# A vision block chain with a selective scan: the last stage of each image moves, through DRAM, into the scan of the next image

## The chip, the core and the metric

The kernel runs on one core of a Trainium2 chip. The time is device microseconds from start to end of one launch, the median of several runs. Five engines work side by side, each through its own instructions in order: PE (matrix multiply; PEld is its weight load), DVE (vector engine), ACT (scalar engine), POOL (GpSimd) and SP, which here only issues DMAs. They wait for one another by semaphores.

## The reference

Eight images of 56 x 56 positions (L = 3136 tokens) with 192 channels go through four blocks, each added to its input. All is float32.

1. A gated unit: group norm, then three projections to 576 channels; two Toeplitz products along the image's rows and columns; the gate; a projection back.
2. Window attention: 7 x 7 windows, shifted by 3, six heads, with a bias table.
3. A 3 x 3 convolution per channel.
4. A two-dimensional selective scan. A projection makes 2 x 384 channels, x and z; x goes through a 3 x 3 convolution and a Silu. The tokens are then scanned in four orders (rows and columns, forwards and backwards), each with 16 states a channel:

```
h[t] = exp(delta[t] * A) * h[t-1] + delta[t] * x[t] * B[t]
y[t] = sum over the 16 states of C[t] * h[t]
```

The four y and D * x are summed. The **last stage** takes this sum: layer norm over the 384 channels, times Silu(z), a projection to 192 channels, and the block's input is added. That is the output.

## The kernel before, in words

A first part (the Toeplitz products, and the first blocks of image 0) takes 3091 us. The rest, 18,104 us, is a single program over the scans of all eight images; all other work is laid between the scan's instructions.

**The scan.** An image has four scan orders, called slots, in the order 2, 3, 0, 1; a slot has seven chunks of 448 tokens (`CH`), a chunk three groups of 128 channels (`d`), a group eight steps `k` of two states each. One step is a *pair*: there are 672 pairs an image and 5,376 in all. The loop over `pairs` writes each one's instructions:

- POOL multiplies du by B into a ring buffer (`inject`, L1124), two pairs ahead;
- ACT makes the decays exp(delta * A) into PSUM (`decay`, L1141, two activations), sets the start values (L1131) and keeps the last states (L1163);
- DVE scans (L1150);
- the result times C (`times_c`, L1156) goes to POOL for even k and to DVE for odd k;
- PE adds the states up with an identity matrix (`add_up`, L1171);
- once per group, DVE adds y into `ysum`, a tile with all tokens of the image (`sums`, L1181 and L1183). It stands at k = 4 of the group after.

SP loads B and C (`load_bc`, L1092), x (`load_xc`, L1097) and delta (`load_delta`) ahead of use.

**The front.** Everything up to the inputs of the scan is the generator `front(b)`: `gate` (block 1), `attention`, `conv2`, `inner` (first projection, convolution and Silu of block 4, in three groups) and `steps` (delta, B and C, in 14 portions of two orders and seven chunks, with a Softplus at L1000). The front of image b + 1 runs while image b is scanned; the next starts as soon as one is through. `gate`, `inner` and `steps` use Silu or Softplus, which need another function table on ACT: a table load stands before and after.

**The finish.** The last stage is the generator `finish(b, j)`, one for each chunk j. It takes `y` straight from `ysum`, makes the mean on PE (L1024), subtracts it on DVE into `yc` in the tile `slab_f` (L1031), and then, for each half of the chunk: the square on ACT (L1036), its mean on PE (L1024), Ln and Exp on ACT (L1041, L1042), a multiply on POOL (L1046), scale and bias on ACT (L1049), a multiply by z on POOL (L1053), the projection on PE (L1058), the sum on DVE (L1066) and the store. SP loads z and the block's input (L1043, L1044) and stores the output (L1067).

**The planner.** `Parts` lays both generators between the pairs. Each yields where it may be put off, with the PSUM banks that it holds and needs (two are free for this) and a time until its load is there. The planner keeps a clock for POOL, ACT, DVE and PE from fixed costs and a list of costs for each kind of client (`"front"`, `"finish"`). After each pair, `step` resumes a client as long as its next piece fits into room that the scan leaves on ACT, PE and DVE (`fits`); a finish is asked before the front. All of this happens when the program is built; the order of each engine is then fixed. Where a piece must be out by some point, the loop calls `parts.step(anything, ...)`, which sets no limits.

**Where the finish stands.** Chunk j of slot 1 is the last part of `ysum` to be complete. Five steps into the chunk after it, the loop forces out what remains of the finish before and adds `finish(pb, pj)`:

```
if i and pslot == 1 and (d, k) == (0, 5):
    while ending in parts.clients:
        parts.step(anything, ending)
    ending = parts.add(finish(pb, pj), "finish")
```

Slot 1 runs backwards, so j goes from 6 to 0, one finish every 24 pairs, from pair 534 of an image to pair 5 of the next. Slot 2 of the next image writes columns across all of `ysum`; at pair 12 the loop therefore forces the last finish on until it has read `ysum` (`while ending.at < 3`).

Of the kernel before, what the change touches and what calls it, by code (L numbers as in the profile page):

```python
# [15 lines left out]
F32 = mybir.dt.float32  # L16
# [7 lines left out]
L = H * W  # L24
# [3 lines left out]
CH = 448  # L28
NCH = L // CH
# [4 lines left out]
ND = DI // 128  # L34
# [5 lines left out]
WP = W + 2  # L40
RUN = 8 * WP
SLOT = NG * (CH + 1) + HALF


class Meter:
# [43 lines left out]
def model(ctx: ExitStack, tc: tile.TileContext, a: dict, out: bass.AP):  # L89
    nc = tc.nc  # L90
    B = out.shape[0]
    const = ctx.enter_context(tc.tile_pool(name="const", bufs=1))
    dram = ctx.enter_context(tc.tile_pool(name="dram", bufs=1, space=DRAM))
# [23 lines left out]
        for n, shape in (("xc", [128, ND, L]), ("bc", [64, L]))  # L117
    )
    dl_d = [[dram.tile([128, ND, L], F32, name=f"dl{s}_{b}") for b in range(B)] for s in range(4)]
    bmask_d = dram.tile([PT_, 4, 6, PT_], F32, name="bmask_d")  # L120
    dg2_d = dram.tile([CP, C // 32, 3, 32], F32, name="dg2_d")
    dg3_d = dram.tile([CP, DI // 32, 3, 32], F32, name="dg3_d")
# [274 lines left out]
    with (  # L397
# [618 lines left out]
        def finish(b, j):  # L1016

            yc, _, sq, rs, x3 = carve(slab_f, 128, (ND, CH), (HALF,), (ND, CH // 2), (CH // 2,), (2, CH // 2))
            x3 = x3[:CP]
            n = CH // 2  # L1020

            def mean(p, src, n):
                for d in range(ND):
                    nc.tensor.matmul(p[:, :n], ones, src[:, d, :], start=d == 0, stop=d == ND - 1)  # L1024

            y = ysum[:, :, j * CH : (j + 1) * CH]
            yield 0, 1
            p = bank()
            mean(p, y, CH)
            yield 1, 0  # L1030
            nc.vector.tensor_sub(yc, y, p[:, :CH].unsqueeze(1).to_broadcast([128, ND, CH]))  # L1031
            for u in range(2):
                yield 0, 0
                tok = slice(j * CH + u * n, j * CH + (u + 1) * n)
                yu = yc[:, :, u * n : (u + 1) * n]
                nc.scalar.activation(sq, yu, AF.Square)  # L1036
                yield 0, 1
                p = bank()
                mean(p, sq, n)
                yield 1, 0  # L1040
                nc.scalar.activation(rs, p[:, :n], AF.Ln, bias=eps5)  # L1041
                nc.scalar.activation(rs, rs, AF.Exp, scale=-0.5)  # L1042
                nc.sync.dma_start(out=sq, in_=z_d[b][:, :, tok])  # L1043
                nc.sync.dma_start(out=x3, in_=blocks(x3_d[b])[:, :, tok])  # L1044
                yield 0, 0
                nc.gpsimd.tensor_mul(yu, yu, rs.unsqueeze(1).to_broadcast([128, ND, n]))  # L1046
                yield 0, 0
                for d in range(ND):
                    nc.scalar.activation(  # L1049
                        yu[:, d, :], yu[:, d, :], AF.Identity, scale=ln_g[:, d : d + 1], bias=ln_b[:, d : d + 1]  # L1050
                    )
                yield 0, 0
                nc.gpsimd.tensor_mul(yu, yu, sq)  # L1053
                yield 0, 1
                p = bank()
                for m in range(2):
                    for d in range(ND):
                        nc.tensor.matmul(  # L1058
                            p[:CP, m * n : (m + 1) * n],
                            w_out[:, d, m * CP : (m + 1) * CP],  # L1060
                            yu[:, d, :],
                            start=d == 0,
                            stop=d == ND - 1,
                        )
                    yield 1, 0
                nc.vector.tensor_add(x3, x3, p[:CP, :CH].rearrange("p (m n) -> p m n", m=2))  # L1066
                nc.sync.dma_start(out=blocks(out[b])[:, :, tok], in_=x3)  # L1067
            yield 0, 0
# [237 lines left out]
        with tc.manual_schedule():  # L1306
            for k in range(NP):
                load_bc(0, k)
            load_delta(0)
            for d in range(ND):  # L1310
                xcs[0, d] = load_xc(0, d)
                times_x(0, d)
            ahead, last = 2, len(pairs) - 1
            parts = Parts()
            run = parts.run

            fed, set_, scanned, taken, summed = ([0.0] * (len(pairs) + ahead + 8) for _ in range(5))

            def feed(g):
                inject(g)  # L1320
                fed[g] = run("P", 1.78, taken[g - 6] if g > 5 else 0.0)

            def take(g):
                times_c(g)
                after = scanned[g], summed[g - 4] if g > 3 else 0.0
                taken[g] = run("P", 1.78, *after) if on_pool(*pairs[g][1:]) else run("D", 1.09, *after)

            def prepare(g):
                decay(g)
                set_[g] = run("A", 1.3, taken[g - 2] if not on_pool(*pairs[g - 2][1:]) else scanned[g - 2])  # L1330

            for g in range(ahead + 2):
                initial(g)
            for g in range(ahead):
                feed(g)
            prepare(0)
            ahead_of, b_next = parts.add(first, "front"), 1
            ahead_of.at, ahead_of.needs = so_far, 1
            ending, anything = None, dict.fromkeys("ADE", 1e9)
            for g, (i, d, k) in enumerate(pairs):  # L1340
                b, slot, j = chunks[i]
                if ahead_of not in parts.clients and b_next < B:
                    ahead_of = parts.add(front(b_next), "front")
                    b_next += 1
                more = i + 1 < len(chunks)
                if more and d == 1 and k == 0:
                    b1, slot1, j1 = chunks[i + 1]
                    while (b1, slot1 // 2, j1) not in made:
                        parts.step(anything, ahead_of)
                    load_delta(i + 1)  # L1350
                    for e in range(2):
                        xcs[i + 1, e] = load_xc(i + 1, e)
                if more and (d, k) == (2, 0):
                    xcs[i + 1, 2] = load_xc(i + 1, 2)
                if more and (d, k) in ((1, 6), (1, 7), (2, 6)):
                    times_x(i + 1, k - 6 if d == 1 else 2)
                    run("P", 0.93)
                pi, pd, pk = pairs[g - 1]
                if g + ahead <= last:
                    feed(g + ahead)  # L1360
                if g and on_pool(pd, pk):
                    take(g - 1)
                if g:
                    keep_state(g - 1)
                    run("A", 0.15, scanned[g - 1])
                if g < last:
                    prepare(g + 1)
                if g + ahead + 2 <= last:
                    initial(g + ahead + 2)
                    run("A", 0.19, taken[g - 2] if g > 1 else 0.0)  # L1370
                scan(g)
                scanned[g] = run("D", 2.02, set_[g], fed[g])
                if not on_pool(d, k):
                    take(g)
                if g and pd == ND - 1 and pi + 1 < len(chunks):
                    load_bc(pi + 1, pk)
                done = (i, d - 1) if d else (i - 1, ND - 1)
                if k == 2 and g > NP and chunks[done[0]][1] == 2:
                    xds[done] = load_xc(*done)
                if i % (4 * NCH) == 0 and b > 0 and (d, k) == (1, 4):  # L1380
                    while ending.at < 3:
                        parts.step(anything, ending)
                if k == 4 and g > NP:
                    sums(*done)
                pb, pslot, pj = chunks[i - 1]
                if i and pslot == 1 and (d, k) == (0, 5):
                    while ending in parts.clients:
                        parts.step(anything, ending)
                    ending = parts.add(finish(pb, pj), "finish")

                n1 = max(parts.t["D"], fed[g + 1], set_[g + 1])
                n2 = n1 + (2.02 if on_pool(*pairs[min(g + 1, last)][1:]) else 3.11)
                parts.step({"A": max(n2, fed[g + 2]) - 0.7, "E": n1 + 5.0, "D": 0.2})
                if g >= 2:
                    add_up(g - 2)
                    summed[g - 2] = run("E", 1.1, taken[g - 2])
            if on_pool(d, k):
                times_c(last)
            for g in (last - 1, last):
                add_up(g)  # L1400
            while parts.clients:
                parts.step(anything)
            sums(i, d)
            drain(finish(b, j))


# [102 lines left out]
```

## Time and profile before

| | |
|---|---|
| median of 3 runs | 21210.55 us (21205.3 to 21239.73) |
| profiled execution, its own time | 21232.23 us |
| its span, first to last instruction | 21230.4 us |
| mean granted PE clock | 0.887 |
| PE busy | 17275.3 us (81%) |
| DVE busy | 15946.5 us (75%) |
| POOL busy | 15628.1 us (74%) |
| ACT busy | 12357.9 us (58%) |
| DMA | 3470.49 MB, mean 163 GB/s |
| scan of images 0 to 6 | 3090.9 to 19334.3 us |
| scan of image 7 | 19334.3 to 21194.7 us |

A line of the profile's groups names the line of the kernel, the engine, the operation, the tile written and those read, the shapes, the number of instructions, their busy time and mean duration, and the idle time of the engine ahead of them with what ended it. A line of the waits says which instruction waited for which, for how long in all, how often, and how long at most. A line of the timeline has start, duration, and in brackets the idle time before. A line for a stretch ends with the granted PE clock, the share of time that the DMA engines were busy, and the rate in GB/s.

### The profile page before, as it was taken

What the parts mean: (1) busy time and instruction counts of PE and PEld (TensorE: products, weight loads), DVE (VectorE), ACT (ScalarE), POOL (GpSimd) and SP (SyncE); (2) the same over time, 40 slices, a digit from 0 to 9 for tenths busy, and PEclk for the clock granted to TensorE, in tenths of its full rate; (3) what the DMA queues carried; (4) which work ended last, traced back from release to release, by engine and by line L of the source; (5) the groups of instructions that cost most, each with busy time, mean ns of one, the idle gap of its engine ahead of it and who ended that gap; (6) DMA issues with size and microseconds to landing.
All of it is one profiled execution on the core that took longest, in us unless ns stands there. A gap on an engine that the chain in (4) does not pass through costs nothing. (4 is left out here: it accounts for less than half of the span.)

```text
span 21230.4 us, 204042 instructions
## 1 busy us (share of the span) xinstructions
PE 17275.3 (81%) x59420; PEld 8921.0 (42%) x59420; DVE 15946.5 (75%) x12633; ACT 12357.9 (58%) x31640; POOL 15628.1 (74%) x9378
## 2 busy tenths in 40 slices
PE   8879669877888788878987898778877898787777
PEld 4667534433443344433543344334433444333333
DVE  2333218986799679977898789867996789779998
ACT  3112236756666566757675667666665767575555
POOL 1222218977788778967897788877886789779999
PEclk9989779988998899988998899988988899888889
DMA  4776665456544655376546654565447554664443
GB/s 99 183 171 159 156 201 164 132 169 187 179 140 139 212 182 150 120 209 194 154 134 183 197 173 130 162 200 171 145 129 218 175 153 129 192 200 147 137 134 128
DMA packets 2562885, 3470.49 MB, mean 163 GB/s; under 512 B 932462, under 2 KB 2514896, under 8 KB 2530930
## 3 DMA queue, kind: packets, MB, share of 16 engines
q1 hardware_dynamic: 2542788, 3340.61, 53.4%
q0 software_dynamic: 18976, 116.82, 1.6%
q8 instruction: 473, 7.75, 0.2%
q14 instruction: 648, 5.31, 0.1%
HBM read 2822.68 MB, written 634.11 MB: 163 GB/s over the span
## 5 line engine op out<-in xcount | busy, mean ns | idle before, releaser
L1171 PE MATMUL ps_y<-hc,ident_sb 128*128 128x448 f32 x21504 | 9973.0, 601 | 772.7 <-POOL hc L1156 694.9
L1124 POOL TENSOR_TENSOR ring<-du,bm 128x896 f32<-128x896 f32 x5376 | 9462.5, 1778 | 677.6 <-ACT ring L1131 381.9
L1141 ACT ACTIVATE ps_a<-delta,A_logs_sb 128x449 f32<-128x449 f32 x10752 | 6860.1, 638 | 378.2 <-DVE ring L1150 122.3
L1171 PEld LDWEIGHTS ps_y<-hc,ident_sb 128*128 128x128 f32 x21504 | 4301.0, 210 | 5071.2 <-issue 3630.9
L1156 POOL TENSOR_TENSOR hc<-ring,cm 128x896 f32<-128x896 f32 x2688 | 4776.2, 1777 | 1946.8 <-DVE ring L1150 914.9
L1150 DVE TENSOR_TENSOR_SCAN ring<-ps_a,ring 128x898 f32<-128x898 f32 x2688 | 5423.9, 2018 | 792.8 <-ACT ps_a L1141 690.0
L1150 DVE TENSOR_TENSOR_SCAN ps_a<-ps_a,ring 128x898 f32<-128x898 f32 x2688 | 5427.6, 2019 | 679.8 <-ACT ps_a L1141 622.8
L1156 DVE TENSOR_TENSOR hc<-ps_a,cm 128x896 f32<-128x896 f32 x2688 | 2934.9, 1092 | 1028.3 <-PE ps_y L1171 798.0
L1163 ACT COPY state<-ps_a 128x2 f32<-128x2 f32 x2687 | 426.8, 159 | 2782.1 <-DVE hc L1156 2773.9
L282 POOL COPY tm<-tr 112x2688 f32<-112x2688 f32 x85 | 406.9, 4791 | 1055.0 <-PE ps_tz L319 507.9
L1131 ACT COPY ring<-state 128x2 f32<-128x2 f32 x4608 | 822.4, 178 | 506.1 <-POOL hc L1156 505.2
L1107 POOL TENSOR_TENSOR du<-delta,xcd 128x448 f32<-128x448 f32 x672 | 661.4, 984 | 360.2 <-DMA xcd<-xc 360.2
L319 PE MATMUL ps_tz<-tzx,tm 112*112 112x112 f32 x4008 | 804.9, 370 | 143.6 <-DMA tzx<-qv 84.2
L319 PEld LDWEIGHTS ps_tz<-tzx,tm 112*112 112x112 f32 x4008 | 760.2, 203 | 174.7 <-issue 107.3
L722 PE MATMUL ps_f<-ident_sb,slab 98*98 98x98 f32 x1344 | 341.3, 327 | 602.5 <-ACT slab L715 602.5
L1163 ACT COPY state<-ring 128x2 f32<-128x2 f32 x2688 | 504.6, 188 | 508.8 <-DVE ring L1150 496.6
L323 DVE COPY tzx<-ps_tz 112x448 f32<-112x448 f32 x501 | 311.5, 623 | 593.9 <-PE ps_tz L319 542.0
L241 ACT ACTIVATE sl<-ps_qv 128x384 f32<-128x384 f32 x600 | 293.3, 491 | 779.5 <-PE ps_qv L240 590.1
L1058 PE MATMUL ps_f<-slab_f,w_out_sb 128*96 128x224 f32 x1320 | 348.7, 408 | 368.9 <-POOL slab_f L1053 366.3
L722 PEld LDWEIGHTS ps_f<-ident_sb,slab 98*98 98x98 f32 x1344 | 203.4, 157 | 1021.2 <-ACT slab L715 802.8
L991 PE MATMUL ps_f<-slab,w_dt_sb 12*128 12x448 f32 x1260 | 441.7, 712 | 219.6 <-ACT slab L983 157.4
L553 PE MATMUL ps_f<-ident_sb,slab 112*96 112x112 f32 x4704 | 529.0, 267 | 110.8 <-DVE slab L561 69.1
(259 smaller groups left out, 17370.3 us busy)
## 6 DMA issues: line engine op xcount, KB each, us to landing
bm<-bc SPq DMA_DIRECT2D x1792, 448.0 KB
cm<-bc SPq DMA_DIRECT2D x1792, 448.0 KB
xcd<-xc SPq DMA_DIRECT2D x840, 224.0 KB
dl<-slab SPq DMA_DIRECT2D x224, 672.0 KB
delta<-dl SPq DMA_DIRECT2D x224, 672.0 KB
tzx<-qv SPq DMA_DIRECT2D x192, 588.0 KB
o<-tzx POOLq DMA_DIRECT2D x192, 588.0 KB, 11.9
slab<-pad SPq DMA_DIRECT2D x483, 232.0 KB
```

The costliest lines, as they stand in the source:

```text
L319: nc.tensor.matmul(po[:, c, :], t[:, c2 + c, :], x[:, :, c1 + c2 + c], start=True, stop=True)
L553: nc.tensor.matmul(p[:CP, t * TT : (t + 1) * TT], ot[:, n % 2, i, t, c % 2 * CP : c % 2 * CP + CP], ident[:TT, :TT], start=i == 0, stop=i ...
L722: nc.tensor.transpose(p[:PT_, e * PT_ : (e + 1) * PT_], S[:, 3 * g + e, :], ident[:PT_, :PT_])
L991: nc.tensor.matmul(held[s][:, :CH], w_dt[row, o, d * 128 : (d + 1) * 128], rc[row, n % 2, :], start=True, stop=True)
L1107: nc.gpsimd.tensor_mul(du[:, 0, :], deltas[i][:, d, 1 : CH + 1], xcs.pop((i, d)))
L1124: nc.gpsimd.tensor_mul(hs[:, :, tokens(i)[0]], dus[i, d].to_broadcast([128, NG, CH]), bms[i, k])
L1131: nc.scalar.copy(in_ring(g)[:, :, tokens(i)[1]], src)
L1141: nc.scalar.activation(dA[:, n, :], deltas[i][:, d, at : at + CH + 1], AF.Exp, scale=negA[:, slot, d, c : c + 1])
L1150: nc.vector.tensor_tensor_scan(h, dA, hs, 0.0, ALU.mult, ALU.add)
L1156: (nc.gpsimd if on_pool(d, k) else nc.vector).tensor_mul(hc, h[:, :, tokens(i)[0]], cms[i, k])
L1163: nc.scalar.copy(states[i][:, d, NG * k : NG * k + NG], h[:, :, tokens(i)[2]])
L1171: nc.tensor.matmul(yps[i, d][:, :CH], ident, hcs[g][:, n, :], start=k + n == 0, stop=k + n == NP + NG - 2)
```

## The change

The finishes of images 0 to 6 no longer stand in the image's own last slot. When a chunk of slot 1 is complete, its part of `ysum` is stored to a DRAM buffer (two buffers, by turns). In the next image, at its pairs 84, 120, 156, 192, 228, 264 and 300, one `finish` of the image before is added, chunks 0 to 6; what remains of the one before is forced out first. Such a finish first loads its chunk from DRAM into `yc` and allows 8.0 us for it; the rest of it is as it was. The wait at pair 12 is gone. Image 7 has no next image: its finishes stay where they were and read `ysum`; they have their own cost list, `"last"`.

```diff
+FINISH, FINISH_EVERY = 84, 36
...
+    y_d = [dram.tile([128, ND, L], F32, name=f"y{q}") for q in range(2)]
...
             y = ysum[:, :, j * CH : (j + 1) * CH]
+            if b < B - 1:
+                y = yc
+                nc.sync.dma_start(out=y, in_=y_d[b % 2][:, :, j * CH : (j + 1) * CH])
+                yield 0, 0, 8.0
             yield 0, 1
             p = bank()
             mean(p, y, CH)
...
-                if i % (4 * NCH) == 0 and b > 0 and (d, k) == (1, 4):
-                    while ending.at < 3:
+                n = g - b * len(pairs) // B - FINISH
+                if b > 0 and n >= 0 and n % FINISH_EVERY == 0 and n // FINISH_EVERY < NCH:
+                    while ending in parts.clients:
                         parts.step(anything, ending)
+                    ending = parts.add(finish(b - 1, n // FINISH_EVERY), "finish")
                 if k == 4 and g > NP:
                     sums(*done)
                 pb, pslot, pj = chunks[i - 1]
                 if i and pslot == 1 and (d, k) == (0, 5):
-                    while ending in parts.clients:
-                        parts.step(anything, ending)
-                    ending = parts.add(finish(pb, pj), "finish")
+                    if pb < B - 1:
+                        tok = slice(pj * CH, (pj + 1) * CH)
+                        nc.sync.dma_start(out=y_d[pb % 2][:, :, tok], in_=ysum[:, :, tok])
+                    else:
+                        while ending in parts.clients:
+                            parts.step(anything, ending)
+                        ending = parts.add(finish(pb, pj), "last")
```

The added lines move the kernel's line numbers: after the change those of the finish from L1031 on, and of the scan, are six higher (the scan is L1156, L1046 is L1052), and the means at L1024 are L1026. The new load is L1031.

## The prediction

> **What bounds the kernel now.** I read the page first (no engine above 81%, and a chain of waits too scattered to name a bound), then how long stretches of the scan take, then who waits inside them. A row of the next view is a stretch: start and end, length, busy time of the scans in it and their number, which is the number of pairs.
>
> ```profile
> 3255.90:19334.20 16078.30, 9345.72 (x4658) 0.90 0.55 167
> 19741.00:20767.10 1026.10, 756.44 (x380) 0.87 0.41 132
> 20773.10:21194.60 421.50, 287.61 (x144) 0.91 0.41 132
> 5565.30:5990.80 425.50, 263.37 (x131) 0.97 0.60 168
> 16859.50:17356.70 497.20, 279.43 (x139) 0.96 0.57 161
> 10523.50:11288.60 765.10, 506.73 (x253) 0.92 0.41 129
> 11288.80:11464.50 175.70, 85.92 (x43) 0.86 0.64 180
> 16038.60:16458.80 420.20, 228.96 (x114) 0.86 0.73 226
> 4629.90:5108.80 478.90, 239.54 (x120) 0.85 0.68 207
> 3096.00:3230.70 134.70, 81.43 (x41) 0.87 0.52 182
> 3230.90:3255.70 24.80, 5.99 (x4) 0.62 1.01 262
> 11898.70:12322.00 423.30, 222.35 (x111) 0.87 0.59 192
> ```
>
> Row 2 is image 7 with neither front nor finish: 1026.1 / 380 = 2.70 us a pair. I call that the floor and count all else as time above it. Row 1, from the first gate to the end of image 6, has 16078 - 4658 x 2.70 = 3502 us above it: seven fronts and 49 finishes. Row 3 holds six finishes alone: 421.5 - 144 x 2.70 = 33 us, 5.5 each.
>
> The other rows show a front's phases, bounded by where their instructions stand among the scalar engine's decays. Gate without a finish (row 4): 425.5 - 131 x 2.70 = 72; with 3.5 of them (row 5): 122, so 14 a finish. Attention (row 6): 82, no finish ever beside it. Conv2 (row 7): 60. Inner without (row 8): 112; with 2.8 (row 9): 155, so 15 each. Steps: half of them without a finish (row 10) 24, the join of three pairs to the next phase (row 11) 17, so 65 in all; with 4.4 (row 12): 124, so 13 each. A straight line through all seven cycles gives gate 75 + 12.6 a finish, inner 119 + 14.1, steps 65 + 14.5; the means of attention and conv2 are 84 and 66. A front alone is then 409 us above the floor, seven are 2863, and 3502 - 2863 = 639 us are the 49 finishes: four stand behind the last front (22 us), the other 45 cost 13.7 each.
>
> Why a finish costs 5.5 alone and 13.7 beside steps: the scalar engine and GpSimd in steps.
>
> ```profile
> 12151.74 0.39 ACT L1042 ACTIVATE slab_f<-slab_f 128x224 f32<-128x224 f32 x1
> 12152.15 1.28 ACT L1000 ACT_TABLE_LOAD   x1
> 12153.44 2.44 ACT L1000 ACTIVATE slab<-slab 128x2688 f32<-128x2688 f32 x1
> 12155.90 1.28 ACT L435 ACT_TABLE_LOAD   x1
> ...
> 12158.58 1.50 ACT L1049 ACTIVATE slab_f<-slab_f,ln_b_sb,ln_g_sb 128x224 f32<-128x224 f32 x3
> ```
>
> ```profile
> 12152.20 1.39 POOL L1046 TENSOR_TENSOR slab_f<-slab_f 128x672 f32<-128x672 f32 x1 [4.76 <-ACT slab_f L1042]
> ...
> 12160.21 1.37 POOL L1053 TENSOR_TENSOR slab_f<-slab_f 128x672 f32<-128x672 f32 x1 [4.89 <-ACT slab_f L1049]
> ```
>
> A Softplus between two table loads (5.0 us) stands in the middle of the finish's chain. GpSimd waits 4.8 and then 4.9 us for the scalar engine, with the scan's own multiplies behind it. The waits of GpSimd in row 12 (four finishes), and in row 3 (six), say the same:
>
> ```profile
> POOL slab_f L1046 <- ACT slab_f L1042: 25.6, 8, 4.8
> POOL slab_f L1053 <- ACT slab_f L1049: 19.9, 4, 5.2
> ```
>
> ```profile
> POOL slab_f L1046 <- ACT slab_f L1042: 0.5, 2, 0.2
> ```
>
> Gate and inner have such blocks too (Silu: 2.45 and 2.82 us between loads of 1.28). Attention has none: its longest scalar instruction, decays aside, is 0.58 us. Busy times there (row 6; PE, PEld, DVE, ACT, POOL):
>
> ```profile
> 10523.50:11288.60 765.10, 633.27 (x2287) 312.91 (x2286) 722.03 (x600) 562.57 (x1779) 691.95 (x413) 0.92 0.41 129
> ```
>
> A pair of 3.02 us has DVE busy 2.85, POOL 2.74, PE 2.50, ACT 2.22: the vector engine is nearly the bound, the others have room.
>
> **The change part by part.**
>
> *Finishes move.* By the changed order of instructions, the seven finishes of images 0 to 5 now stand at pairs 84 to about 330 of the next image, nearly all beside its attention, which stretches from 253 pairs to 273-283. Steps shrink from about 107 pairs to 83, a whole cycle stays near 654, and the last front ends at pair 4591 instead of 4618; with a front's cost counted above the floor, these pairs need no term. Each finish issues what it did: POOL 2 x (1.381 + 1.375) = 5.5 us, ACT 2 x (0.761 + 0.446 + 0.391 + 3 x 0.563) = 6.6, DVE 1.55 + 2 x 0.61 = 2.8, PE 11.8, and six DMAs. Of the 42, two fall into gate (12.6 each = 25); the seven of image 6 go into image 7 at 5.5 = 38. The price of the other 40 is the unknown. Low end 1.5: attention's room over 36 pairs (POOL 10 us, DVE 6) swallows the finish, and only the 28 added pairs run at attention's 0.32 above the floor (9 us over six). High end 14.5, as in steps. I take 6.5: the free 5.5, as there are no long scalar blocks, plus 1 because attention's own reduction waits on the scalar engine that now has 6.6 us more. So 40 x 6.5 + 25 + 38 = 323 against 639: **-316 us**. Ends: 40 x 1.5 gives -516, 40 x 14.5 gives +4.
>
> *A store and a load through DRAM.* 49 of each, 672 KB, 67 MB beside 3470 (1.9%). In the DMA records the equal loads delta<-dl land 6.3 us after issue (middle 80%: 4.7 to 8.8), the equal stores dl<-slab after 5.5, at most 8.8. The planner gives y 8.0 us before its first matmul, so I take 0; if each were 2.9 late (the longest load, 10.9) and PE stood, 142. The store waits on SP for an add issued one pair earlier; behind it on SP stand the front's transfers, later delta and bm. SP waits 6.4 us a time for the softplus output already (677 us in 105), so I take 0, at most one pair each, 132. The first sum of the next image overwrites ysum and must wait for the last store, seven pairs (19 us) behind its issue: 10 to spare; 0, and if SP comes 18 late as it does at its worst, 8 x 7 = 56.
>
> *Planner waits removed* (a finish forced out before the next; the first three parts forced at pair 12): the second half was out 11 to 21 pairs after the first, within the 24, so 0. They order instructions only.
>
> *Two rules of the Trainium skill* stand against parts of this and the sum does not use them. TensorE: Matmul & The Clock Gate (Architectural detail) says that ScalarE, VectorE and GpSimdE are strict FIFO, so a finish's hops between engines would hold what is behind them wherever it stands: 40 x 13.7 + 63 = 611, a gain of only 28. Against it row 3 shows the same hops at 5.5. ScalarE: Activation LUTs (What ACT_TABLE_LOAD costs) puts a switch at 2.66 us with a drain; the Softplus block would be 2 x 2.66 + 2.44 = 7.8 us, and escaping it worth 2.7 us more a finish, some 120 in all. The trace shows 5.0 and no drain, so I leave that out.
>
> **Sum.** The profiled execution took 21232.2 us (span 21230.4): 21232 - 316 = 20916. The median of the runs is 22 below it: **20895**, 1.5% faster. About 0.2%, 42 us, can be told from no change.
>
> **The rivals.**
> 1. *Forecast*, 0.52: 20895.
> 2. *The finish stalls itself*, 0.14: 13.7 each in attention too, 28 gained, 21183. For: PE waits at L1058 for POOL in row 3 as well (37.2 us in six finishes). Against: DVE waited 13 us for PE in all six.
> 3. *Slower: the vector engine becomes the bound in attention*, 0.08. Its reductions hang on scalar and PE, and PE can stand at L1058 up to 7.7 us twice a finish. If both stand on the path: 5.5 + 15.4 = 20.9 each, 40 x 20.9 + 63 = 899, 21471. It decides from (639 - 63) / 40 = 14.4 on. For: DVE 94% busy. Against: room on PE.
> 4. *Steps get no cheaper*, 0.14: they move data at a DMA share near 0.6 and now run in 83 pairs. If their base is 90 (what the last cycle shows with 2.5 finishes, these free), seven times 25 comes back: 21070.
> 5. *Attention swallows it*, 0.12: 1.5 each, 20695.
>
> **How the numbers follow.** Cases 1, 4, 5 and half of 2 are faster by over 0.2%: 0.85; the rest of 2 and of the DMA prices is the same, 0.06; 0.09 slower. The range, 20720 to 21180, leaves out most of 5 and 3 and ends at 2; the forecast's own is 20800 to 21000.
>
> **What would show it.** Right: steps near 83 pairs in 290 us, the waits of L1046 and L1053 on ACT mostly gone, attention with finishes at 3.0 to 3.25 us a pair (at 6.5 each: 280 pairs in about 880), image 7 near 1900 instead of 1860. Wrong: attention above 3.4 a pair, which eats the gain; new waits of DVE for y's store, or of PE for its load; steps still above 3.6 a pair.

## The result, and the profile after

The changed kernel takes 21321.69 us (median of 4 runs, 21316.9 to 21351.62), the kernel before 21214.93 us beside it. The ratio is 1.0051, with a 95% interval of 1.0034 to 1.0069: **slower by half a per cent, some 107 us**, where 1.5% faster was forecast. The profiled execution took 21316.9 us (before: 21232.2).

The first view answers the table of stretches in the prediction: start and end, length, busy time of the scans and their number, which is the number of pairs or one more (a scan that begins just at the edge is counted). It is the changed kernel's.

```profile
3247.97:19017.98 15770.01, 9117.59 (x4545) 0.89 0.56 171
20297.09:20848.81 551.72, 406.14 (x205) 0.85 0.41 134
8073.58:9064.65 991.07, 603.15 (x301) 0.90 0.45 136
14891.41:15911.14 1019.73, 607.09 (x303) 0.89 0.43 131
9605.21:9917.87 312.66, 172.19 (x86) 0.83 0.65 216
19556.15:20221.86 665.71, 429.45 (x216) 0.85 0.44 141
```

Row 1 is all seven fronts: 15770 - 4545 x 2.70 = 3498 us above the floor. Before it was 3474, and 3502 with the four finishes behind the last front. The floor has not moved either (row 2: 551.72 over 204 pairs is 2.70). So seven fronts with 42 finishes beside them cost 24 us more than seven fronts with 45. Rows 3 and 4 are two attentions with their finishes: 3.29 and 3.37 us a pair, where 3.0 to 3.25 was forecast. Row 5 is steps with no finish beside it, 3.64 a pair. Row 6 is image 7 from its pair 84 to 300, with six moved finishes and no front: 665.71 - 216 x 2.70 = 82 us, 13.7 each, where such finishes had cost 5.5.

The waits of the changed kernel (total us, times, longest; three engines and SP's queue) say what is new in the finish:

```profile
POOL slab_f L1052 <- ACT slab_f L1048: 102.7, 49, 11.8
POOL slab_f L1059 <- DMA slab_f<-z: 79.0, 21, 6.9
POOL slab_f L1059 <- ACT slab_f L1055: 50.2, 36, 4.2
...
PE ps_f L1026 <- DMA slab_f<-y: 171.6, 25, 12.4
...
DVE slab_f L1037 <- PE ps_f L1026: 189.9, 32, 13.6
...
SPq L1049 <- PE ps_f L1026: 1370.7, 83, 47.6
```

The same waits in the kernel before:

```profile
POOL slab_f L1046 <- ACT slab_f L1042: 292.1, 80, 10.4
POOL slab_f L1053 <- ACT slab_f L1049: 158.1, 47, 5.2
POOL slab_f L1053 <- DMA slab_f<-z: 31.1, 19, 3.6
...
DVE slab_f L1031 <- PE ps_f L1024: 88.2, 38, 4.9
...
SPq L1043 <- PE ps_f L1024: 969.3, 101, 26.7
```

GpSimd's two waits for the scalar engine fell as forecast: 292.1 us to 102.7, and 158.1 to 50.2. In their place PE now waits for the load of y (171.6 us in 25 waits, up to 12.4), the vector engine for PE's mean behind it (189.9, before 88.2), and GpSimd for z (79.0, before 31.1). The last line of both views is SP's: its load of z waits for the finish's mean on PE up to 47.6 us (before 26.7), with every later load of B, C, x and delta queued behind it.

How such a wait for y comes about, in image 7 at its pair 120 (start, duration, engine, and in brackets the idle time before it):

```profile
19666.03 0.36 SPq L1098 DMA_DIRECT2D cm<-bc  x1
19666.44 0.47 SPq L1098 DMA_DIRECT2D bm<-bc  x1
19667.01 0.41 SPq L1098 DMA_DIRECT2D cm<-bc  x1
19667.52 0.52 SPq L1031 DMA_DIRECT2D slab_f<-y  x1
...
19675.84 4.85 PE L1026 MATMUL ps_f<-slab_f,ones 128*128 128x448 f32 x6 [10.91 <-DMA slab_f<-y]
...
19680.73 1.55 DVE L1037 TENSOR_TENSOR slab_f<-slab_f,ps_f 128x1344 f32<-128x1344 f32 x1 [9.04 <-PE ps_f L1026]
...
19684.35 1.77 POOL L1162 TENSOR_TENSOR hc<-ring,cm 128x896 f32<-128x896 f32 x1 [9.71 <-PE ps_y L1177]
```

SP has just got through the loads of B and C for the chunk, and only then issues the load of y. The mean is next in PE's own order, 8.3 us after the issue, as soon as the data are there. PE stood for 10.9 us, and with it the scan: the vector engine waited 9.0 us, GpSimd 9.7.

The planner does allow 8.0 us for a load, but here the allowance is void: the generator yields it as the first thing that it does, and a new `Entry` has `ready = 0.0`, so `at + sum(load)` is 8.0 us on a clock that has run for thousands of them. The mean is laid one pair behind the load. Where SP had run 7 to 11 pairs ahead of the scan, the load was still early enough. That is so for 23 of the 28 loads in the middle of a chunk (pairs 84, 156, 228, 300: offset 12 in chunks of 24 pairs); for the other five, all beside a front, SP was 0 to 2 pairs ahead, and PE waited for four of them. At the start of a chunk (120, 192, 264: offset 0) PE waited for all 21: SP is level with the others there, because it issues a chunk's loads of B and C from about pair 17 to 24 of the chunk before, as their buffers come free.

### The profile page after: what moved, and what is told of

Read it like the earlier page. It is cut to its first block, busy times and chain, and to the rows that moved or that the text cites. A ratio compares the mean times of both kernels' runs of the same rounds, so it can differ in the third digit from the quotient of the medians.

```text
span 21315.1 us, 204418 instructions
## 1 busy us (share of the span) xinstructions
PE 17297.9 (81%) x59420; PEld 8946.0 (42%) x59420; DVE 15932.6 (75%) x12633; ACT 12355.6 (58%) x31640; POOL 15615.2 (73%) x9378
## 5 line engine op out<-in xcount | busy, mean ns | idle before, releaser
L1156 DVE TENSOR_TENSOR_SCAN ring<-ps_a,ring 128x898 f32<-128x898 f32 x2688 | 5421.0, 2017 | 827.7 <-ACT ps_a L1147 621.1
L1156 DVE TENSOR_TENSOR_SCAN ps_a<-ps_a,ring 128x898 f32<-128x898 f32 x2688 | 5428.7, 2020 | 626.3 <-ACT ps_a L1147 540.1
L244 DVE TENSOR_TENSOR qv<-sl 128x576 f32<-128x576 f32 (+1 forms) x200 | 196.4, 985 | 552.4 <-ACT sl L243 548.0
```

The lines of the kernel that those rows point to most:

```text
L1156: nc.vector.tensor_tensor_scan(h, dA, hs, 0.0, ALU.mult, ALU.add)
```

## The experiments

Three theories were on trial, and the expectations go by these letters:
- **A, the load of y is late**: PE stands for it in finishes that start with a chunk.
- **B, attention is dear by itself**: its own use of the engines makes a finish there cost some 12 us, whatever the load does.
- **C, the queue of SP**: a finish that starts in the middle of a chunk has its second load of z among the loads of B and C, so z, B or C come late.

To compare fronts, I cut each trace at the front's phases, as in the prediction, and count the time above 2.70 us a pair over seven cycles. "Finishes" is the whole sum above that of the kernel with no finish of images 0 to 6 (the ninth experiment), divided by 49.

| kernel | time us | ratio to before, 95% | gate | attention | conv2 | inner | steps | image 7 | a finish |
|---|---|---|---|---|---|---|---|---|---|
| before | 21214.9 | 1 | 645 | 588 | 463 | 923 | 855 | 46 (+28 tail) | 10.1 |
| changed | 21321.7 | 1.0051 (1.0034 to 1.0069) | 595 | 1058 | 433 | 859 | 554 | 139 | 11.9 |
| no load of y | 21114.1 | 0.9941 (0.9925 to 0.9958) | 565 | 913 | 439 | 867 | 559 | 108 | 8.1 |
| no load, no store | 21094.2 | 0.9936 (0.9919 to 0.9952) | 563 | 908 | 435 | 854 | 565 | 109 | 7.8 |
| allowance counted | 21212.4 | 0.9992 (0.9982 to 1.0001) | 590 | 995 | 447 | 832 | 543 | 136 | 10.0 |
| load 12 pairs early | 21100.6 | 0.9938 (0.9923 to 0.9953) | 571 | 902 | 443 | 857 | 551 | 105 | 7.7 |
| 77, every 48 | 21042.9 | 0.9910 (0.9896 to 0.9925) | 582 | 874 | 486 | 830 | 514 | 95 | 6.7 |
| early, 72 every 48 | 21004.9 | 0.9897 (0.9883 to 0.9912) | 560 | 820 | 499 | 869 | 510 | 95 | 6.1 |
| early, 84 every 48 | 21104.7 | 0.9943 (0.9929 to 0.9958) | 569 | 893 | 484 | 844 | 523 | 119 | 7.7 |
| early, 77 every 48 | 21067.4 | 0.9923 (0.9908 to 0.9938) | 595 | 860 | 496 | 842 | 504 | 110 | 7.2 |
| early, 120 every 24 | 21148.4 | 0.9952 (0.9937 to 0.9967) | 558 | 948 | 499 | 850 | 522 | 91 | 8.5 |
| early, 96 every 24 | 21084.0 | 0.9919 (0.9904 to 0.9934) | 553 | 897 | 440 | 851 | 555 | 97 | 7.0 |
| no finishes | 20747.3 | 0.9765 (0.9748 to 0.9782) | 519 | 604 | 454 | 830 | 597 | 48 | 0 |

The last three kernels ran beside a median of 21260.1 for before (the others beside 21215 to 21227), so ratios compare them better than times. The phases are of one profiled execution each; for "early, 72 every 48" it was the slowest run, 36 us above the median, and for "no finishes" the fastest, 27 us below (by the ratios of the medians a finish at 72 every 48 is (0.9897 - 0.9765) x 21215 / 49 = 5.7).

**1. The load left out.** The finish reads `ysum` in place of the loaded chunk, which by then holds other sums; the order of the instructions stays, and so do the stores.

```diff
-                y = yc
-                nc.sync.dma_start(out=y, in_=y_d[b % 2][:, :, j * CH : (j + 1) * CH])
                 yield 0, 0, 8.0
```

> The changed kernel with the load from DRAM left out: a moved finish reads ysum, which by then holds partial sums of the next image (so the data are not the reference's); the stores stay, and so do the places of all finishes. Theory A (the load is late: its 8.0 us count from a clock that stands at zero, so the first mean is laid one pair behind the load, and PE stands 7 to 8 us where SP had not run ahead, 25 times of 49, 172 us of PE waits): the late ones cost some 6.5 us more than the others in image 7, so about 160 us come back, 21160 us. Theory B (a finish beside attention is dear by itself): no change, 21300 to 21340. Theory C (SP's queue: the loads of z stand among the loads of B and C and hold them up): little, 21280 to 21330.

21114.1 us: 1.1% below the changed kernel, and below before. Attention falls from 1058 to 913 us, image 7 from 139 to 108. So the load is worth more than the whole loss (the 33 MB that it moves are gone too), and B can at most explain what remains above the free price.

**2. The allowance made to count**, from the planner's clock at the time when the finish is added.

```diff
                 entry = Entry(work, costs.setdefault(name, []))
+                if name == "finish":
+                    entry.ready = max(self.t.values())
```

> The changed kernel, but a new finish starts with its ready time at the planner's present clock, so that the 8.0 us for the load count from now and the mean is laid two to three pairs later. Theory A: PE's waits for the load fall from 172 us to under 50, time 21160 to 21220. Theories B and C: 21300 to 21340.

21212.4 us, the same as before (0.9982 to 1.0001): a good half of the load's price came back. The fault in the allowance is real, but it is not all of A. In the waits of this kernel PE still stands for y, 63.8 us in 15 waits in place of 171.6 in 25:

```profile
PE ps_f L1026 <- DMA slab_f<-y: 63.8, 15, 7.2
```

The planner counts the 8.0 us from where the load stands in the program; it does not know that SP comes to it late. Nor is 8.0 us always enough: by the records of the semaphores that a DMA raises when it lands, the loads that PE still waited for landed 6.0 to 11.4 us after their issue.

**3. The load 12 pairs ahead of the finish.**

```diff
+                e = n + 12
+                if b > 0 and e >= 0 and e % FINISH_EVERY == 0 and e // FINISH_EVERY < NCH:
+                    while ending in parts.clients:
+                        parts.step(anything, ending)
+                    q = e // FINISH_EVERY
+                    nc.sync.dma_start(
+                        out=carve(slab_f, 128, (ND, CH))[0], in_=y_d[(b - 1) % 2][:, :, q * CH : (q + 1) * CH]
+                    )
...
-                nc.sync.dma_start(out=y, in_=y_d[b % 2][:, :, j * CH : (j + 1) * CH])
-                yield 0, 0, 8.0
+                yield 0, 0
```

> The changed kernel, the load from DRAM issued 12 pairs (some 36 us) before its finish is added, all else in place. Theory A: no wait of PE for the load is left, time as without the load, 21160. Theory B: 21300 to 21340. Theory C: 21300, as the loads of z stand where they stood.

21100.6 us, as fast as with no load at all (0.9923 to 0.9953 against 0.9925 to 0.9958). No wait of PE for y is left, and the vector engine's wait for the mean is down from 189.9 us to 19.4:

```profile
DVE slab_f L1036 <- PE ps_f L1026: 19.4, 17, 1.8
```

Two stretches of 17 pairs in image 7, where nothing but the scan and one finish runs, show which finishes paid. First the changed kernel at offset 12 (pair 156) and offset 0 (pair 120):

```profile
19779.42:19835.08 55.66, 33.88 (x17) 0.88 0.61 190
...
19666.56:19724.88 58.32, 33.80 (x17) 0.82 0.34 109
```

then the kernel with the early load, at offset 12 (pair 84) and offset 0 (pair 120):

```profile
19372.17:19428.74 56.57, 33.90 (x18) 0.85 0.59 187
19482.57:19533.31 50.74, 33.80 (x17) 0.90 0.36 111
```

Above 17 x 2.70 = 45.9 us, offset 0 went from 12.4 to 4.8, offset 12 stayed at 10 to 11. The other finishes of image 7 agree, over 17 pairs from each one's start: at offset 0 the changed kernel has 12.4, 18.1 and 17.7 us, with the load early 4.4 to 4.9, without it 3.0 to 5.0; at offset 12 all three kernels have 8.8 to 12.5. **A is shown, and it sits in the finishes that start with a chunk** (153 of the 172 us for which PE waited for y; the four waits at offset 12 are the rest). The places of all fronts and finishes are the same in the three kernels. The other finishes have another price.

**4. No load and no store.** As the first, and the store of `ysum` left out too.

```diff
-                        tok = slice(pj * CH, (pj + 1) * CH)
-                        nc.sync.dma_start(out=y_d[pb % 2][:, :, tok], in_=ysum[:, :, tok])
+                        pass
```

> The run without the load, and the stores to DRAM left out as well (the data are again not the reference's): what do 49 stores cost? Steps were forecast at 65 us above the floor a front without finishes and came out at 79. If the store holds SP, and the front's transfers behind it, steps fall by 14 x 7 = 98 us: 21015. If it costs nothing, as the prediction has it, 21114 as without the load.

21094.2 us against 21114.1 without the load alone. 20 us, 0.4 a store, and the intervals overlap: the store is as good as free. It is not what makes steps dearer than forecast (565 us here, 559 with the store).

**5. Other places: 77, every 48 pairs**, the load as in the changed kernel.

```diff
-FINISH, FINISH_EVERY = 84, 36
+FINISH, FINISH_EVERY = 77, 48
```

> The changed kernel with its finishes at pairs 77, 125, 173 and so on, 48 apart: each starts at the fifth step of a chunk, where SP has run ahead, and both its loads of z are out before SP comes to the loads of B and C for the next chunk (pairs 17 to 24 of a chunk). Theory A: the load from DRAM is issued early, PE's waits for it go, 21160. Theory B: 21300 to 21340. Theory C: the waits for z and for B and C go as well; a finish then costs some 6 us as it did behind the last front in the kernel before, and the time falls to 20900 to 21050.

21042.9 us, 1.3% below the changed kernel by a change of two constants. All finishes start five pairs into a chunk, where SP is some pairs ahead (PE waits for y 24.6 us in all), and their loads of z are out before those of B and C begin. What a finish that starts at offset 12 meets instead is seen in the changed kernel's order of time at pair 156 of image 7:

```profile
19805.67 0.41 SPq L1073 DMA_DIRECT2D out_dram<-slab_f  x1
19806.13 0.71 SPq L1098 DMA_DIRECT2D bm<-bc  x1
19806.90 0.49 SPq L1098 DMA_DIRECT2D cm<-bc  x1
19807.50 0.63 SPq L1049 DMA_DIRECT2D slab_f<-z  x1
...
19815.89 1.37 POOL L1059 TENSOR_TENSOR slab_f<-slab_f 128x672 f32<-128x672 f32 x1 [4.20 <-DMA slab_f<-z]
...
19817.32 2.56 PE L1064 MATMUL ps_f<-slab_f,w_out_sb 128*96 128x224 f32 x6 [8.81 <-POOL slab_f L1059]
...
19819.97 2.03 DVE L1156 TENSOR_TENSOR_SCAN ring<-ps_a,ring 128x898 f32<-128x898 f32 x1 [2.24 <-POOL ring L1130]
```

The second load of z is issued behind loads of B and C (which wait for their buffers), GpSimd's multiply by z comes 8.4 us after it and has waited 4.2, PE 8.8, and the next scan waits for GpSimd.

**6, 7, 8. The early load at three offsets**, all every 48 pairs: 72 (offset 0), 84 (offset 12), 77 (offset 5). The edit is the third's, with other constants.

```diff
-FINISH, FINISH_EVERY = 84, 36
+FINISH, FINISH_EVERY = 72, 48
```

> The load issued 12 pairs early, and all finishes at pairs 72, 120, 168 and so on, 48 apart: each starts with a chunk. Theory C (what is left is SP: a finish whose loads of z fall among the loads of B and C, pairs 17 to 24 of a chunk, gets z late): in image 7 of the run with the early load the finishes that start with a chunk cost 6 us and those that start at its pair 12 cost 11 us; with 28 of 49 moved from the dear place to the cheap one, 5.5 x 28 = 154 us under that run's 21101: 20950. Theory B (attention is dear wherever in the chunk the finish starts): 21070 to 21130.

> The same, all finishes at pairs 84, 132, 180 and so on, 48 apart: each starts at pair 12 of a chunk and its second load of z stands among the loads of B and C. Theory C: 21 of 49 moved from the cheap place to the dear one, 5.5 x 21 = 115 us above the run with the early load: 21215, about the time before the change, and GpSimd's waits for z rise above 100 us. Theory B: 21070 to 21130.

> The same, all finishes at pairs 77, 125, 173 and so on, 48 apart: each starts at pair 5 of a chunk as in the kernel before. Against the run with these places and the load as the change has it (21043), only PE's 25 us of waits for the load can go: Theory A 21018. Theory C: no wait for z, as there.

Offset 0 gives 21004.9 us, the fastest of all: 1.0% faster than before and 1.5% faster than the changed kernel. Offset 12 gives 21104.7, where C had 21215, and offset 5 21067.4, where A had 21018. Offset 12 lies inside the range that B had for it (21070 to 21130); offset 0, for which B had the same, lies between C's 20950 and that range, and 65 us below it. GpSimd's wait for z, of the kernel at offset 0

```profile
POOL slab_f L1058 <- DMA slab_f<-z: 4.4, 4, 2.0
```

and of the one at offset 12:

```profile
POOL slab_f L1058 <- DMA slab_f<-z: 150.5, 36, 7.9
```

The two differ in nothing but 12 pairs, and 100 us lie between them: 2.0 a finish, beside 3.0 of GpSimd's waits for z. So C is right in direction. By the semaphore records it is two things: at offset 12 the second load of z is issued 2.4 us (median) after the mean that frees its buffer, at offset 0 0.07; and it lands 7.3 us after its issue in place of 3.7. The order on SP is the smaller part, slower landing the larger; in the stretches above the DMA engines are busy 0.59 to 0.61 of the time at offset 12, 0.34 to 0.36 at offset 0. The size of C is not what the stretches of image 7 let one expect (5 us more at offset 12 than at 0, hence the expected 21215): beside a front less than half of it reaches the end. Nor are all of the 100 us shown to be C's, as the fronts fall elsewhere in their chunks too; in image 7, where no front runs, they are 119 - 95 = 24 us, 3.4 a finish. And offset 5, without waits for z (9.6 us), is still 62 us dearer than offset 0; there slot 2's loads of x come in (the sums wait 91.8 us for them, at offset 0 55.2), which accounts for part of it at most. With the early load offset 5 is not better than without (21042.9), so an early load only helps where the load was late, and the place among the loads of B and C is the other part of the matter.

B falls. With the load early and the offset 0, the whole price of a finish is 5.7 us (medians) to 6.1 (profiled executions), the former good to about 1 us, and so near the 5.5 that the prediction had read from the finishes of image 7. An attention with such finishes, in the kernel at offset 0, is at 3.19 us a pair (934.53 over 293 pairs), against 3.29 and 3.37 in the changed kernel:

```profile
10265.63:11200.16 934.53, 587.06 (x293) 0.91 0.45 140
```

**9. No finishes at all** for images 0 to 6, nor their loads and stores (their outputs are not made; image 7's own finishes stay). It gives the fronts' base.

```diff
-                    while ending in parts.clients:
-                        parts.step(anything, ending)
-                    ending = parts.add(finish(b - 1, n // FINISH_EVERY), "finish")
+                    pass
```

> Leaves out the finishes of images 0 to 6 with their stores and loads of y (their outputs are not made); the fronts, the scan and image 7's own finishes stay. It gives the fronts' true base, which the prediction took from straight lines through before's cycles. If those lines were right (gate 75, attention 84, conv2 66, inner 119, steps 65, a front 409): phases over seven cycles of 525, 588, 462, 833 and 455 us above the floor, image 7 at 46, and 21215 - 639 + 22 (the tail's four, which are left out here) - 22 = about 20575 us. If steps cost 79 a front without any finish, as they do in every kernel that moves the finishes: steps near 553, and about 20670 us. If the steps are dear only because a delayed front meets them elsewhere in the slots: steps vary with the last front's end and stand between, 480 to 520.

20747.3 us, a ratio of 0.9765. The stretch of all fronts is 14808 - 4371 x 2.70 = 3006 us above the floor (3004 by the phases):

```profile
3234.78:18042.49 14807.71, 8769.17 (x4371) 0.89 0.56 170
```

All 49 finishes are worth 512 us in the profiled executions (21232.2 - 20720.1), not 639. Of these, 24 lie ahead of the scan, which begins that much earlier here; by the table they are 496, 10.1 each, by the medians 10.2. The straight lines through before's cycles were right for gate (519 for 525), attention (604 for 588), conv2 (454 for 462) and inner (830 for 833). They were wrong for steps: 597 us, 85 a front, where they gave 65. One cycle's steps in this kernel, first half, second half and the join to the next gate:

```profile
9266.40:9419.76 153.36, 82.12 (x41) 0.84 0.59 204
9419.76:9558.46 138.70, 81.91 (x42) 0.84 0.60 201
9558.46:9585.30 26.84, 6.09 (x4) 0.62 0.99 273
```

41 pairs with 42.7 us above the floor, 41 with 28.0, three with 18.7: 89. The prediction had doubled one half, the second half of image 0's steps (24), because no other half in before's trace was free of finishes. In these two halves the waits show PE for the scalar engine's copy before the projections of delta:

```profile
PE ps_f L993 <- ACT slab L985: 30.7, 12, 3.6
```

Why the first half (the column orders) is dearer than the second, the runs do not tell. Nor is 85 a fixed figure: a cycle of this kernel is 624 pairs, 26 chunks, so all its steps from the second image on start at the same offset in a chunk (13). With finishes the offsets vary, and steps cost 72 to 81 a front.

**10, 11. Closer together: 120 every 24 and 96 every 24**, with the early load, so that all finishes start with a chunk and none stands behind attention.

```diff
-FINISH, FINISH_EVERY = 84, 36
+FINISH, FINISH_EVERY = 120, 24
```

> The load of y 12 pairs early, as in the kernel with finishes at 72 and every 48, but here at 120, 144, ... 264: all seven still start with a chunk, and lie closer. Late load and full SP queue (mechanism by mechanism): no finish stands in gate or past attention any more, so 42 in attention at 5.5 each (attention 820 us above the floor), conv2 back from 499 to about 463, gate from 560 to about 545; 21005 - 50 = about 20955 us. If finishes that stand closer disturb one another (the vector engine is 94% busy there): more than 7 each in attention, above 880, and 21005 to 21080 us, no better than every 48.

> The same, one chunk earlier: 96, 120, ... 240. One finish of each image falls into gate (12.6 by before's line, beside Silu blocks and table loads) in place of attention (5.5): by the place alone six times 7 = 40 us slower than 120 and every 24, about 20995 us. If the place in gate costs nothing once y is there early, the same as that kernel within 20 us.

21148.4 and 21084.0 us; by the ratios 117 and 47 us behind offset 0 every 48. Both are dearer, as the rival of crowding has it, and the place in gate did not count: fewer finishes fall there than expected (the fronts drift ahead of the images, and from image 3 on the finish at pair 96 stands in attention too), and the kernel that has them is the faster of the two. In one attention, the waits of PE for GpSimd's multiply by z, at 120 every 24

```profile
PE ps_f L1063 <- POOL slab_f L1058: 41.7, 13, 6.5
```

and at 72 every 48:

```profile
PE ps_f L1063 <- POOL slab_f L1058: 26.5, 10, 4.9
```

But the first has seven finishes in it and the second six, and over the whole kernels the same wait is 261.1 and 253.0 us: this wait is not what 117 us are made of. One cause is at hand, though not separated from mere density: with the load 12 pairs ahead into the same tile, what is left of the finish before must be forced out within 12 pairs. The 65 us between these two kernels stand in conv2 (499 against 440) and attention, and conv2 holds no finish in either. What differs there is where it falls within a chunk. Both kernels have the same distance between finishes, so these 65 us are not crowding, and how much of the 117 and 47 is crowding the runs do not show.

## Why the prediction was wrong

Its sum was -316 us; the scan became 91 us longer. The miss of 407, by its own terms (against the kernel without finishes):

| term | forecast | measured | miss |
|---|---|---|---|
| removed: 45 finishes beside fronts | -617 | 3474 - 3004 = 470 | +147 |
| removed: four behind the last front | -22 | -27 | -5 |
| added: finishes in attention | +260 | 1058 - 604 = 454 | +194 |
| added: in gate, and the other phases' change | +25 | 41 | +16 |
| added: seven in image 7 | +38 | 139 - 46 = 93 | +55 |

**The step that failed first** is "The planner gives y 8.0 us before its first matmul, so I take 0". The number stands in the diff, but I did not follow it into `resume` and `Entry`, where `at` is 0.0 for a new client. In its place PE waited 171.6 us in 25 waits, 6.9 each. The upper end that I kept, 142 us for 49 loads 2.9 us late, was too low for the same reason: it took for granted that 8 of the 10.9 us were covered. Without the load the kernel is 184 us (profiled) to 208 us (medians) faster, 7 to 8 for each of the 25 late loads. I did name the sign to look for, "of PE for its load", as what would make the forecast wrong; it is the line with 171.6 us.

**The term for attention** (6.5 each for 40) measured 11.4 as changed; by the trace 38 of the 42 begin in attention and four in gate, not two, so rather 11.9. With the load out of the way it goes down to (913 - 604) / 38 = 8.1, and at offset 0 with 48 pairs between to (820 - 604) / 32 = 6.8, with 5.7 to 6.1 for a finish over the whole kernel. So the 6.5 was about right for a finish away from Silu and Softplus blocks, if its loads are on time. I priced what the engines do and not where the finish's loads meet the queue of SP; of SP's queue I had only asked what the store would delay. Image 7 fails for the same two reasons: 13.3 instead of 5.5 each, 8.9 without the load, 7.0 at offset 0.

**The credit for the old place** was 13.7 a finish and is 10.1 to 10.4. The step is "half of them without a finish (row 10) 24, the join of three pairs to the next phase (row 11) 17, so 65 in all". That the straight line agreed with it was luck: both extrapolate to steps without a finish from a trace that has almost none. This is rival 4 ("their base is 90") by most of its size: 79 in the changed kernel, 85 with no finishes.

**What held.** Steps shrank to 85 pairs in 299 to 321 us (forecast 83 in 290), gate and inner got cheaper, the waits of GpSimd for the scalar engine fell by 297 us, the floor and the store behaved as said. On PE the late load shows what order costs: the scan's own additions stood behind the mean for 10.9 us, though they needed nothing from it. The rule of strict FIFO that the prediction weighed (the Trainium skill, TensorE: Matmul & The Clock Gate, Architectural detail) names ScalarE, VectorE and GpSimdE; of PE it says only that weight loads can be pulled ahead of matmuls. Nor is the order alone the price: a finish with the same hops costs 5.7 to 6.1 us where its data are there.

The outcome is neither of my rivals by itself, but most of rival 2 (11.4 to 11.9 of its 13.7 in attention), most of rival 4 and the dearer image 7 together. I had priced them one at a time, and each alone left a gain.

## What to carry to other kernels

When work that used to read on-chip data is made to load it, follow the load through its queue: count how far ahead of its first reader it stands in the program, what the queue's engine is doing at that point, and what the planner's allowance is counted from. A load with a dozen pairs of lead was free here, and the same load one pair ahead cost some 7 to 8 us whenever its queue was not already ahead. And where a term is "what the old place cost", look for the place without the thing that is removed; if the trace has none, the intercept of a line is a guess, and it wants its own range.

## What the runs showed beyond that

- A load of 672 KB that is issued by a queue level with the engines held PE for 6.9 us on average over 25 waits, 12.4 at most (10.9 in the case above). By the semaphore records the 49 loads of y landed 4.4 to 10.3 us after their issue, 19 of them after more than 8.0, so landing time, not the queue's 0.5 us per issue, is the price.
- The place within a chunk matters for the front too. In 91 conv2 phases of 13 kernels, those that begin at pairs 3 to 8 of a chunk cost 56 us above the floor on average (16 of them), those at 12 to 20 cost 73 (29). Over seven cycles that can be 50 to 100 us, as much as the finishes' offset. So single phases of two kernels are not to be compared closer than some 30 us, and a kernel whose cycle gets longer or shorter can get dearer or cheaper where nothing was edited. These bands were picked after the fact and the cause was not tried; B and C are loaded at the end of a chunk.
